# The last 32 nodes of a range as four products of 96 columns, joined by identity weights (graph network layer, one core)

## Chip, core and metric

The kernel runs on one core of one Trainium2 chip. The metric is the device time of one execution in microseconds; of several runs the median is used. The engines are TensorE (PE, its weight loads are PEld), VectorE (DVE), ScalarE (ACT), GpSimd (POOL) and SyncE (SP). SP computes nothing and issues most transfers.

## What is computed

A message-passing layer with two edge types, then a residual, then a layer normalisation over 6250 nodes of 128 features and 100000 edges, sorted by destination:

```python
Xs = X[src]
m_data = Xs @ W_data.T + b_data
m_ctrl = Xs @ W_control.T + b_control
msg = jnp.where((edge_types == 0)[:, None], m_data, m_ctrl)
agg = jax.ops.segment_sum(msg, dst, num_segments=X.shape[0])
out = agg + (X @ W_self.T + b_self)
x = _layernorm(x + relu(out), axis=-1)
```

All of it is float32 outside; the result is x.

## The kernel before

**The table.** In the first 56 us the kernel computes both messages of every node, and splits each float32 message into three bf16 parts of 128 columns (384 columns, `D3`) whose sum is the message. They stay on the chip as `m3` (98 blocks of 128 rows) and are written to memory as `table`.

**Windows.** 4320 nodes are treated in 27 windows of 160 nodes (`WN`). A window has up to 2688 edges (21 columns of 128). `ranks` sorts its edges by the table block of their source: it makes one-hot matrices (`hots`, L691), and products with `every` (all ones), `tri` and `rest` (L702) count them, so that each edge gets a slot; the list that comes out (`vs`) is written to memory as `packed` (L772) and read back for each window as `rows` (L904), spread over all partitions. Edges that find no slot are listed apart and gathered from the table (`sr`, `gl`).

**Steps.** For each window, `sums` runs 25 steps g. Stage 1 (L933): four products take 32 messages each out of four blocks of m3 into PSUM `g`, 384 columns. A cast (L436, on ACT, a few on DVE) makes `gs` of it, in bf16. Stage 2 adds the 128 messages to their nodes in the PSUM bank `a`, with a one-hot matrix `hot2` of 160 columns as weights: four products (L947) for nodes 0 to 127 of the window, 32 nodes each into partitions 32j to 32j+31, 384 columns. A bank has 512 columns, so 128 are left beside those 384 for nodes 128 to 159. Three products (L950) of 128 columns with the same 32 weights put the three bf16 parts there, one part into each of three strips of 32 partitions. At the end of the window ACT copies that corner, 96 partitions x 128 columns, into `bs`.

**Closes.** After the windows of a group (groups of 1, 2, then six times 4 windows) `close` adds the three parts (L561, on DVE), the node's own product (L518, f32) and bias (L521), and does the residual and the normalisation. The last 32 nodes of up to four windows are put together as one block of rows `f`. There one product per window (L552) adds the three parts by a 96x32 weight `fold`, three identity matrices above each other, in f32.

**Gathered nodes.** The other 1930 nodes go another way: GpSimd gathers their messages from the table, 128 edges at a time (`t_msg`, L1027, 263 of these), and TensorE adds them with one-hot weights (L1034, bank `ga`, four products of 384 columns). These sets stand between the steps of the windows.

**Order.** All instructions are entered into a `Plan` with an engine, a duration, a due time and dependences. The planner then lays them out on a model of the engines, by readiness and due time, and emits each engine's instructions in that order. The durations given to it decide only the order. `slack` on an operation makes it ready later in the plan, so that it stands further back in its queue; SP operations of some kinds have it (`packed_b` 2.0), but only when due after 60 us (`FROM`).

Of the kernel before, what the change touches and what calls it, by code (L numbers as in the profile page):

```python
# [10 lines left out]
F32 = mybir.dt.float32  # L11
# [5 lines left out]
SP = mybir.EngineType.SP  # L17
# [4 lines left out]
P = 128  # L22
D = 128
D3 = 3 * D
# [19 lines left out]
R = 32  # L44
# [203 lines left out]
def sums_over_windows(ctx, tc, x, xt, edges, w, bias, out, total):  # L248
    nc = tc.nc
    V, A, G, T, S = nc.vector, nc.scalar, nc.gpsimd, nc.tensor, nc.sync  # L250
    dram = ctx.enter_context(tc.tile_pool(name="dram", bufs=1, space=DRAM))
    const = ctx.enter_context(tc.tile_pool(name="consts", bufs=1))
    work = ctx.enter_context(tc.tile_pool(name="work", bufs=2))
# [3 lines left out]
    add = plan.add  # L257
# [4 lines left out]
    def B(pool, shape, dtype, name, bufs=1, room=None):  # L262
        return Buf(plan, pool, shape, dtype, name, bufs, room)

    def C(shape, dtype, name):
        return Buf(plan, const, shape, dtype, name, 1)

    XC = 4 * WN
    T0 = 36.0
    TW = 13.0  # L270
    LAT = 0.1
# [2 lines left out]
    SPD = 0.45  # L274
# [6 lines left out]
        lat=4.0)  # L281
    w_sb = C([D, D3], F32, "w_sb")
# [14 lines left out]
    def vec(due, cols, fn, r, w, rate=1.04):  # L297
        return add("DVE", dve(cols, rate), fn, due, r, w)
# [11 lines left out]
    ident = C([P, P], F32, "ident")  # L310
# [31 lines left out]
        [tri_f], [rest])  # L342
    every = C([P, P], BF16, "every")
    vec(4, P, lambda: V.memset(every.t, 1.0), [], [every], 0.3)
    fold = C([3 * R, R], F32, "fold")
    vec(30, R, lambda: V.tensor_add(fold.t, ident.t[: 3 * R, 0:R], ident.t[: 3 * R, R : 2 * R]),
        [ident], [fold])
    vec(30, R, lambda: V.tensor_add(fold.t, fold.t, ident.t[: 3 * R, 2 * R : 3 * R]),
        [ident, fold], [fold])
    minus = C([P, P], BF16, "minus")  # L350
    vec(1.5, P, lambda: V.tensor_scalar_mul(minus.t, ident.t, -1.0), [ident], [minus])
    wbase = C([P, NW], I32, "wbase")
# [123 lines left out]
    for q in range(NS):  # L476
        bs = range(2 * q, min(2 * q + 2, NB))
        nb = len(bs)
        due = 4.0 + MS * q
# [44 lines left out]
    def close(tag, n0, step, rows, sums_a, block, due, queues=("SP",)):  # L524
# [12 lines left out]
        if block:  # L537
            xb = B(work, [D, len(block), W4], F32, "xb", 2, 4 * W4)
            b0, b1_ = block[0][0] - P, block[-1][0] + R
            for j, (at, _) in enumerate(block):  # L540
                add("SP", SPD, lambda at=at, j=j: S.dma_start(
                    xr.t[R * j : R * j + R, nw, :], x[at : at + R, :]), due - 20, late,
                    [(xr, ("x", nw + j))], lat=2.5)
            add("SP", SPD, lambda: S.dma_start(
                xb.t, xt[:, b0:b1_].rearrange("d (b p) -> d b p", p=WN)[:, :, P:]), due - 20, late,
                [xb], lat=2.5)
            f = low()

            def mms():
                o = lambda j, m: f.t[R * j : R * j + R, :D]  # L550
                for j, (_, bs) in enumerate(block):
                    T.matmul(o(j, R), fold.t, bs.t, start=True, stop=False, skip_group_check=True)  # L552
                own(o, lambda j, m: xb.t[:, j, :], mb)
            add("PE", 0.6, mms, due, [xb, w_sb, one3, brows, fold] + [b for _, b in block], [f])
        mv = B(work, [P, nb, 2], F32, "mv" + tag, 2, 10)
        for k in range(nb):
            if k < nw:
# [63 lines left out]
    def ranks(gi, w0, nw, when, step, engines):  # L621
# [75 lines left out]
                        op=ALU.is_equal), [st1, iota1_b], [hkey(k)], 0.52)  # L697
        wide = nw * NT

        def add_to(c, wt, k, start, stop):  # L700
            for j in range(4):
                T.matmul(acc.t[R * j : R * j + R, c * wide : c * wide + wide],  # L702
                         wt.t[:, R * j : R * j + R], one(k).rearrange("p w c -> p (w c)"),
                         start=start, stop=stop, skip_group_check=True)
        mine = lambda r: [(c, c * L + r) for c in range(nc_) if c * L + r < min(KT, c * L + L)]
        for k in range((nc_ - 1) * L):
            add("PE", (nc_ - 1 - k // L) * wide / 2400, lambda k=k: [
                add_to(c, every, k, k == 0 and c == 1, False) for c in range(k // L + 1, nc_)], when + 1.5,
                [hkey(k), every], [acc])
        for r in range(L):  # L710
            due = when + 2 + step * r
            m = mine(r)
# [57 lines left out]
        def put():  # L770
            if both:
                S.dma_start(packed[gi, :both].rearrange("h p c -> p h c"), vs.t[:, :both])  # L772
            if both < nh:
                S.dma_start(packed[gi, both, :64], vs.t[:64, both])
        add("SP", SPD, put, d2 + 1, [vs], [(packed_b, gi)], lat=2.0)
        to_d = B(work, [P, nw, NS, 2], BF16, "to_d", 2, 4 * NS * 2)
        for t in range(4):
            nx = NS if t < 2 else NS - 1
# [115 lines left out]
    def sums(gi, w0, nw, placed):  # L894
# [5 lines left out]
        for i in range(nw):  # L900
# [25 lines left out]
            for g in range(NS):  # L926
# [18 lines left out]
                def stage2(g=g, gs=gs, a=a, hot2=hot2, last=last):  # L945
                    for j in range(4):
                        T.matmul(a.t[R * j : R * j + R, :D3], hot2.t[:, g, R * j : R * j + R],  # L947
                                 gs.t, start=g == 0, stop=False, skip_group_check=True)
                    for c in range(3):
                        T.matmul(a.t[R * c : R * c + R, D3:], hot2.t[:, g, P:],  # L950
                                 gs.t[:, c * D : (c + 1) * D], start=False, stop=last,
                                 skip_group_check=True)
                add("PE", 0.22, stage2, d + 0.9, [gs, (hot2, (g >= 9) + (g >= 17))], [a])
                if g == 12:
                    def own_a(i=i, a=a, xc=xc):
                        own(lambda j, m: a.t[R * j : R * j + R, :D],
                            lambda j, m: xc.t[:, i * WN + R * j : i * WN + R * j + R], P)
                    add("PE", 0.3, own_a, d + 1, [xc, w_sb, one3, brows], [a])
            bs = B(work, [3 * R, D], F32, "bs", 5)
            evict(lambda bs=bs: bs.t, lambda a=a: a.t[: 3 * R, D3:], D, due + TW + 0.8, [a], [bs])  # L960
            got.append((w0 + i, a, due + TW + 0.8, bs))
        return got

# [263 lines left out]
```

## Time and profile before

| | |
|---|---|
| median of 14 runs | 481.54 us (476.09 to 488.06) |
| profiled execution | 482.4 us, span 480.8 us |
| granted TensorE clock, mean | 0.989 |
| TensorE busy 0 to 12 us / 12 to 60 / 60 to 180 / 180 to 420 / 420 to 460 | 5.6 of 12 / 47.8 of 48 / 107.9 of 120 / 233.4 of 240 / 39.6 of 40 us |
| VectorE busy 60 to 180 / 180 to 420 / 420 to 460 | 107.8 of 120 / 209.3 of 240 / 21.3 of 40 us |
| L950: records | 1944 with gs and 81 with gl |
| L436: casts of gs | 639, 481 ns each |
| L1027: gathers | 263, 1073 ns each |

A line of the groups reads: line, engine, operation, output<-inputs, (partitions x elements, type), xcount | busy us, mean ns of one | idle us of the engine just before them, and what ended it. `128*32` is the part of TensorE's array that a product uses, rows by outputs. Products are pipelined: the next begins before the one before has ended, so their durations overlap. A line of the chain or the timeline reads: start us, duration us, engine and line, xcount, and in brackets the idle time before it. An f32 product is two records.

### The profile page before, as it was taken

Reading aid. Unit: us, or ns where it says so; the run is one execution under the profiler, and the core shown is the slowest. Engines: PE = TensorE matmul, PEld = TensorE weight load, DVE = VectorE, ACT = ScalarE, POOL = GpSimd, SP = SyncE. Lnnn points to the kernel's source line nnn. Section 1 sums busy time; section 2 is a strip of 40 time slices with the busy share of each in tenths; the row PEclk is TensorE's granted clock in tenths of the full one; section 3 lists DMA queues with packets and bytes.
Section 4 is the critical chain, followed back from the end, with each engine's and each line's share of the span. In section 5 each row is a group of like instructions: output and inputs, shape, how many; then the busy total and the mean of one; then the engine's idle time right before and its main releaser. Section 6 shows DMA issues by size and latency. Waiting matters only on the chain.

```text
span 480.8 us, 26926 instructions
## 1 busy us (share of the span) xinstructions
PE 443.3 (92%) x11461; PEld 362.0 (75%) x11461; DVE 394.5 (82%) x1271; ACT 354.2 (74%) x891; POOL 302.1 (63%) x290
## 2 busy tenths in 40 slices
PE   4999978997999799999999999999999999999990
PEld 3666556775888578788887879888888888888970
DVE  6699979998999958999988898888978779564342
ACT  2475765765877777778886789877887778989981
POOL 1100028777777777777777775777777757777700
PEclk9999999999999989999999999999999999999996
DMA  5479977428463646642766435753366534646210
GB/s 146 126 246 358 291 238 187 119 77 279 130 187 79 201 109 204 173 137 72 232 186 169 111 110 181 202 188 104 81 218 186 170 76 111 218 150 187 79 52 20
DMA packets 63117, 76.83 MB, mean 160 GB/s; under 512 B 21000, under 2 KB 52893, under 8 KB 62989
## 3 DMA queue, kind: packets, MB, share of 16 engines
q1 hardware_dynamic: 49147, 47.35, 31.3%
q0 software_dynamic: 13456, 27.42, 21.1%
q8 instruction: 91, 1.49, 1.3%
q10 hardware_dynamic: 386, 0.26, 0.2%
q14 instruction: 37, 0.30, 0.2%
HBM read 60.50 MB, written 13.17 MB: 153 GB/s over the span
## 4 chain that ended last, share of the span: by engine, by line
PE 75%; DVE 8%; ACT 7%; DMA 6%; issue 2%; ACTq 0%; DVEq 0%; POOLq 0%
PE g L933 21%; PE a L947 20%; PE rk L702 8%; PE ga L1034 7%; ACT gs L436 3%; PE a L950 3%; PE g L493 3%; PE vt L752 3%; DMA t_msg<-table,t_idx 2%; DMA rows<-packed 2%; DVE slot L716 2%; PE a L493 2%; ACT to_d L443 2%; DVE hot L920 2%; PE ga L702 1%
## 5 line engine op out<-in xcount | busy, mean ns | idle before, releaser
L1027 POOL DMA_INDIRECT t_msg<-table,t_idx x263 | 282.3, 1073 | 132.4 <-DVE hots L691 45.3
L436 ACT CAST gs<-g 128x384 bf16<-128x384 f32 x639 | 274.2, 481 | 77.6 <-PE g L933 53.3
L947 PE MATMUL a<-gs,hot 128*32 128x384 bf16 x2592 | 250.1, 330 | 7.8 <-ACT gs L436 5.0
L933 PE MATMUL g<-m,rows 128*32 128x384 bf16 x2646 | 254.6, 328 | 2.0 <-DVE rows L912 1.1
L933 PEld LDWEIGHTS <-rows 128*32 128x32 bf16 x2646 | 167.9, 135 | 14.3 <-issue 1.8
L950 PE MATMUL a<-gs,hot 128*32 128x128 bf16 x1944 | 158.4, 219 | 0.0
L947 PEld LDWEIGHTS <-hot 128*32 128x32 bf16 x2700 | 115.6, 95 | 34.4 <-issue 15.3
L1034 PE MATMUL ga<-t_msg,t_hot 128*32 128x384 bf16 x1036 | 101.5, 328 | 4.3 <-DMA t_msg<-table,t_idx 4.2
L716 DVE TENSOR_REDUCE slot<-rk 128x4 f32<-128x392 f32 (+1 forms) x138 | 76.6, 555 | 14.7 <-PE rk L702 11.7
L950 PEld LDWEIGHTS <-hot 128*32 128x32 bf16 x2025 | 81.2, 97 | 3.6
L920 DVE TENSOR_TENSOR hot<-iota_b,to_d 128x1280 bf16<-128x1280 bf16 (+1 forms) x81 | 67.4, 843 | 0.0
L702 PE MATMUL rk<-hots,tri 128*32 128x392 bf16 (+1 forms) x588 | 59.8, 317 | 0.0
L702 PE MATMUL rk<-hots,rest 128*32 128x392 bf16 (+1 forms) x556 | 54.3, 320 | 4.0 <-DVE slot L716 4.0
L1034 PEld LDWEIGHTS <-t_hot 128*32 128x32 bf16 x1036 | 49.4, 97 | 9.4 <-issue 6.0
L912 DVE TENSOR_SCALAR rows<-rows,pid 128x1568 bf16<-128x1568 bf16 x54 | 35.2, 657 | 8.1 <-DMA rows<-packed 8.0
L691 DVE TENSOR_TENSOR hots<-iota_b,st 128x784 bf16<-128x784 bf16 (+1 forms) x83 | 39.1, 489 | 0.2
L1021 DVE TENSOR_TENSOR t_hot<-iota_b,t_code 128x768 bf16<-128x768 bf16 (+2 forms) x47 | 24.6, 524 | 14.4 <-PE ga L1034 14.3
L702 PEld LDWEIGHTS <-rest 128*32 128x32 bf16 x624 | 24.7, 96 | 13.1 <-issue 10.7
L561 DVE TENSOR_REDUCE s<-a 128x128 f32<-128x384 f32 x27 | 15.0, 557 | 23.8 <-ACT bs L436 11.8
L702 PEld LDWEIGHTS <-tri 128*32 128x32 bf16 x672 | 28.1, 97 | 2.1
L752 PEld LDWEIGHTS <-two 128*64 128x64 bf16 x567 | 14.4, 109 | 8.5 <-DVE two L743 3.3
L861 POOL DMA_INDIRECT sr<-table,at x14 | 15.8, 1126 | 4.3 <-issue 2.4
(188 smaller groups left out, 531.6 us busy)
## 6 DMA issues: line engine op xcount, KB each, us to landing
rows<-packed SPq DMA_DIRECT2D x27, 784.0 KB
table<-m SPq DMA_DIRECT2D x12, 768.0 KB
t_msg<-table,t_idx POOLq DMA_INDIRECT x263
rows<-in_xt SPq DMA_DIRECT2D x8, 256.0 KB
xc<-in_xt SPq DMA_DIRECT2D x6, 320.0 KB
gl<-sr SPq DMA_DIRECT2D x27, 48.0 KB
xr<-in_x SPq DMA_DIRECT2D x5, 256.0 KB
out<-xr SPq DMA_DIRECT2D x5, 256.0 KB
```

The costliest lines, as they stand in the source:

```text
L436: [("ACT", act(cols), lambda: A.copy(o(), src())), ("DVE", dve(cols), lambda: V.tensor_copy(o(), src()))], None, None, due, r, w, lat)
L691: lambda k=k, kn=kn, ci=ci, hs4=hs4: V.tensor_tensor(hv(ci)[:, k - ks[ci] : k - ks[ci] + kn].rearrange("p k w (c d) -> p (k w) c d", d=2), ...
L702: T.matmul(acc.t[R * j : R * j + R, c * wide : c * wide + wide], wt.t[:, R * j : R * j + R], one(k).rearrange("p w c -> p (w c)"), start=s ...
L716: vec(due, len(m) * wide, lambda r=r, m=m: V.tensor_reduce(slot.t[:, r:KT:L, :], acc.t[:, : len(m) * wide].rearrange("p (k w c) -> p k w c ...
L752: T.matmul(vv()[q : q + 64, i // 2, :], two.t[:, (k - k0) * nw + i].rearrange("p f r -> p (f r)"), one(k)[:, i, :], start=k == 0 and i < 2 ...
L912: add("DVE", dve(half * NT, 0.335), lambda sp=sp, rs=rs: V.tensor_scalar(sp.t[:, rs], sp.t[:, rs], pid1.t, None, op0=ALU.is_equal), due - ...
L920: lambda i=i, hot2=hot2, s4=s4, c0=c0, c1=c1: V.tensor_tensor(hot2.t[:, c0:c1].rearrange("p g (c d) -> p g c d", d=2), iota1_b.t.rearrange ...
L933: T.matmul(gp.t[R * t : R * t + R, :D3], sp.t[:, :, 4 * g + t], m3.t[:, 4 * g + t, :], start=True, stop=True)
L947: T.matmul(a.t[R * j : R * j + R, :D3], hot2.t[:, g, R * j : R * j + R], gs.t, start=g == 0, stop=False, skip_group_check=True)
L950: T.matmul(a.t[R * c : R * c + R, D3:], hot2.t[:, g, P:], gs.t[:, c * D : (c + 1) * D], start=False, stop=last, skip_group_check=True)
L1027: add("POOL", GC, lambda m=m, kk=kk: G.indirect_dma_start(out=m.t, out_offset=None, in_=table[:, :], in_offset=bass.IndirectOffsetOnAxis(a ...
L1034: T.matmul(ga.t[R * i : R * i + R, :D3], hot.t[:, k % KB, R * i : R * i + R], m.t, start=k == 0, stop=False, skip_group_check=True)
```

## The change

It has four parts.

1. Stage 2 puts the last 32 nodes as four products of 96 columns (`Q = D3 // 4`) into all four strips of 32 partitions, instead of three of 128 columns into three strips. So 96 of the 128 columns beside the 384 are used, on all 128 partitions. `bs` is [128, 96].
2. In `close` the parts no longer lie one under the other with the same columns: a quarter of 96 columns crosses the borders between the parts of 128. Each block takes six f32 products, with the 32 columns of the identity matrix `ident` that select a strip as weights, of 96, 32, 64, 64, 32 and 96 columns. `fold` and its two VectorE instructions go.
3. The products with `every` for one one-hot matrix, one for each of up to three chains, become one product that reads the same columns up to three times.
4. The put of `packed` for group 1 gets a slack of 3.0 in the plan. Two durations in the plan change: stage 2 from 0.22 to 0.206, the close's products from 0.6 to 1.0.

```diff
+    Q = D3 // 4
...
-    fold = C([3 * R, R], F32, "fold")
-    vec(30, R, lambda: V.tensor_add(fold.t, ident.t[: 3 * R, 0:R], ident.t[: 3 * R, R : 2 * R]),
-        [ident], [fold])
-    vec(30, R, lambda: V.tensor_add(fold.t, fold.t, ident.t[: 3 * R, 2 * R : 3 * R]),
-        [ident, fold], [fold])
...
-                for j, (_, bs) in enumerate(block):
-                    T.matmul(o(j, R), fold.t, bs.t, start=True, stop=False, skip_group_check=True)
+                first_ = True
+                for at in sorted({*range(0, D3, Q), *range(0, D3, D)}):
+                    q, f0 = at // Q, at % D
+                    n = min(Q - at % Q, D - f0)
+                    for j, (_, bs) in enumerate(block):
+                        T.matmul(f.t[R * j : R * j + R, f0 : f0 + n],
+                                 ident.t[:, R * q : R * q + R],
+                                 bs.t[:, at % Q : at % Q + n], start=first_, stop=False,
+                                 skip_group_check=True)
+                    first_ = False
                 own(o, lambda j, m: xb.t[:, j, :], mb)
-            add("PE", 0.6, mms, due, [xb, w_sb, one3, brows, fold] + [b for _, b in block], [f])
+            add("PE", 1.0, mms, due, [xb, w_sb, one3, brows, ident] + [b for _, b in block], [f])
...
-        def add_to(c, wt, k, start, stop):
+        def add_to(c, wt, k, start, stop, n=1):
             for j in range(4):
-                T.matmul(acc.t[R * j : R * j + R, c * wide : c * wide + wide],
-                         wt.t[:, R * j : R * j + R], one(k).rearrange("p w c -> p (w c)"),
-                         start=start, stop=stop, skip_group_check=True)
+                T.matmul(acc.t[R * j : R * j + R, c * wide : (c + n) * wide].rearrange(
+                    "p (n c) -> p n c", n=n), wt.t[:, R * j : R * j + R],
+                    one(k).rearrange("p w c -> p (w c)")[:, None, :].to_broadcast([P, n, wide]),
+                    start=start, stop=stop, skip_group_check=True)
...
         for k in range((nc_ - 1) * L):
-            add("PE", (nc_ - 1 - k // L) * wide / 2400, lambda k=k: [
-                add_to(c, every, k, k == 0 and c == 1, False) for c in range(k // L + 1, nc_)], when + 1.5,
-                [hkey(k), every], [acc])
+            more = nc_ - 1 - k // L
+            add("PE", max(more * wide / 2400, 0.08), lambda k=k, more=more: add_to(
+                nc_ - more, every, k, k == 0, False, more), when + 1.5, [hkey(k), every], [acc])
...
-        add("SP", SPD, put, d2 + 1, [vs], [(packed_b, gi)], lat=2.0)
+        op = add("SP", SPD, put, d2 + 1, [vs], [(packed_b, gi)], lat=2.0)
+        if gi == 1:
+            op.slack = 3.0
...
-                    for c in range(3):
-                        T.matmul(a.t[R * c : R * c + R, D3:], hot2.t[:, g, P:],
-                                 gs.t[:, c * D : (c + 1) * D], start=False, stop=last,
+                    for c in range(4):
+                        T.matmul(a.t[R * c : R * c + R, D3 : D3 + Q], hot2.t[:, g, P:],
+                                 gs.t[:, c * Q : c * Q + Q], start=False, stop=last,
                                  skip_group_check=True)
-                add("PE", 0.22, stage2, d + 0.9, [gs, (hot2, (g >= 9) + (g >= 17))], [a])
+                add("PE", 0.206, stage2, d + 0.9, [gs, (hot2, (g >= 9) + (g >= 17))], [a])
...
-            bs = B(work, [3 * R, D], F32, "bs", 5)
-            evict(lambda bs=bs: bs.t, lambda a=a: a.t[: 3 * R, D3:], D, due + TW + 0.8, [a], [bs])
+            bs = B(work, [P, Q], F32, "bs", 5)
+            evict(lambda bs=bs: bs.t, lambda a=a: a.t[:, D3 : D3 + Q], Q, due + TW + 0.8, [a], [bs])
```

In the queues this gives: SP's put of `packed` for group 1 stands behind the third of the small xr loads (L541), and not ahead of the first xr load; both reads of `rows` of group 1 remain behind it, past one xb and one t_xc load. From 60 us on places change in all queues; GpSimd's gathers keep their order, and sr reads shift by one to three places among them.

## The prediction

> **What bounds the kernel now.** I read the page first, then the chain of waits, the waits, the timeline of three stretches, and the busy time by stage.
>
> ```profile
> span 480.8 us, 26926 instructions
> PE 443.3 (92%) x11461; PEld 362.0 (75%) x11461; DVE 394.5 (82%) x1271; ACT 354.2 (74%) x891; POOL 302.1 (63%) x290
> PE 75%; DVE 8%; ACT 7%; DMA 6%; issue 2%; ACTq 0%; DVEq 0%; POOLq 0%
> L947 PE MATMUL a<-gs,hot 128*32 128x384 bf16 x2592 | 250.1, 330 | 7.8 <-ACT gs L436 5.0
> L950 PE MATMUL a<-gs,hot 128*32 128x128 bf16 x1944 | 158.4, 219 | 0.0
> ```
>
> TensorE is busy for 92% of the span and holds 75% of the chain. The mean of 219 ns of L950 is no price, since four such products run beside each other and one follows another before it ends. The price is read from starts, in the timeline of PE in a dense stretch:
>
> ```profile
> 444.31 0.44 PE L947 MATMUL a<-gs,hot 128*32 128x384 bf16 x4
> 444.69 0.43 PE L947 MATMUL a<-gs,hot 128*32 128x384 bf16 x4
> 445.02 0.48 PE L1034 MATMUL ga<-t_msg,t_hot 128*32 128x384 bf16 x4
> 445.23 0.44 PE L947 MATMUL a<-gs,hot 128*32 128x384 bf16 x4
> 445.61 0.43 PE L947 MATMUL a<-gs,hot 128*32 128x384 bf16 x4
> ```
>
> A step g (four L933, four L947, three L950) takes 0.38 us; with a gathered set (L1034, four products of 384 columns) between, 0.54. So a set of four times 384 columns costs 0.16 us, which is 0.417 ns a column, and a step is 384 + 384 + 128 columns: 0.16 + 0.16 + 0.055 = 0.375. Three of the four strips of 32 outputs carry all 896 columns; the fourth has 768. The change takes the three full strips to 864.
>
> But not all of the span is of this kind. Three pieces of the chain between 157 and 169 us, then a line of the waits (total, times, longest, in us) and one of GpSimd's timeline:
>
> ```profile
> 157.43 3.96 DMA t_msg<-table,t_idx
> 161.55 6.97 DMA t_msg<-table,t_idx
> 168.57 0.35 PE ga L1034 x4
> PE ga L1034 <- DMA t_msg<-table,t_idx: 4.2, 3, 3.4
> 68.25 1.03 POOL L1027 DMA_INDIRECT t_msg<-table,t_idx  x1 [45.34 <-DVE hots L691]
> ```
>
> GpSimd issues its first gather at 68.25 us, after the table has landed, and from there one every 1.3 to 1.4 us with 0.30 between; at 168.57 TensorE has stood 3.37 us for one of them. Whatever TensorE saves before 168.6 is lost in this wait. After it the chain (180 to 468 us) has L933 28.6%, L947 26.6%, L1034 10.0%, L702 9.0%, L950 4.0%, L752 3.1% and a few small ones of TensorE: some 85%.
>
> **The change, part by part.**
>
> *Four products of 96 columns (L950).* L950 has 2025 records with all its forms, three a step, and 1572 of them start after 168.6: 524 steps of the 675. Each step gives 32 columns x 0.417 = 13.3 ns on the strips that set the pace. 524 x 13.3 = 7.0 us; 85% of that, the share of TensorE in the chain there, is 5.9. The 151 steps before give 2.0 us into the wait of 3.37: nothing. A fourth weight load and product a step land on the strip that had room. Is a product of 96 columns with its own weights really shorter than one of 128? The nearest row has 98 columns:
>
> ```profile
> 16.32 0.36 PE L702 MATMUL ga<-xr,rest 128*32 128x98 bf16 x16
> 16.51 0.35 PE L702 MATMUL ga<-xr,tri 128*32 128x98 bf16 x16
> ```
>
> Four sets of four in 0.19 us: 47 ns a set, with sixteen weight loads, against 55 for 128. So the saving lies between 8 ns (this rounded row: 4.2 us after 168.6, 3.6 on the chain) and 13.3; I take 13.3, since the columns of the larger sets are exact to 1%.
>
> The Trainium skill speaks against it: "TensorE: Matmul & The Clock Gate", section "Back-to-back issue gap", gives about 81 ns for each matmul of 128 columns in a stream where every matmul has its own weight load. Were that the floor here, 96 columns would gain nothing and the fourth product might cost. The trace has 55 ns for 128 columns with a load each, so the rule's figure doesn't hold for these narrow strips. By the page the sum would be no gain here, and 483.7 us with the closes.
>
> *ScalarE's pace.* A cast of gs costs 0.39 us in a run of six (2.44 us at 464.72: less the 0.48 of the last, over five). That is more than a step without a gathered set, so where several such steps follow one another ScalarE sets the pace and 0.367 instead of 0.38 buys nothing. With one gathered set to three steps it is 3 x 0.38 + 0.16 = 1.30 for TensorE, 1.17 for ScalarE. ScalarE was busy for 43.3 of the last 48 us, 48 of 60 before. For this and VectorE's like waits I give back 0.9 us (bounds 0 and 3).
>
> *The identity products (L552).* Before, a close sends one f32 product of 128 columns for each block of 32 rows, four strips beside each other. The nearest price is L518, also f32, 128 columns, four strips: 0.22 us for its eight records on the chain at 426.37. After, each block takes six products with 96, 32, 64, 64, 32 and 96 columns: 384 columns, 0.66 us, 0.44 more for a close. There are seven closes with such a block, first records at 115, 182, 243, 302, 361, 420 and 468 us. The first lies before the wait. The last is hidden: TensorE has finished vt at 469.02 and VectorE takes it up at 469.85, after the sums of the last window, so 0.8 us cover it; without that cover it is 0.44 too. Five count: 2.2 us. Bounds: nothing, if they fall into waits; and if none of the twelve weight loads of a strip (110 ns each in the row of L552) hides behind a short product, 12 x 0.11 + 0.66 - 0.22 = 1.76 a close, 8.8 for five and 1.0 at the end. L518's 0.22 for two loads and two products has the loads hidden, so I stay near the first.
>
> *Fewer products with ones.* 36 sets of 98 columns become 18 of 98 to 294, the same columns. By the 47 ns of a 98-column set against its 41 ns of columns, 18 x 6 = 0.1 us at most, before 26 us, so ahead of the wait at 168.6: nothing.
>
> *The put of group 1 and the table.* SyncE's queue before:
>
> ```profile
> 62.17 0.33 SPq L772 DMA_DIRECT2D packed<-vs  x1
> 62.60 0.38 SPq L534 DMA_DIRECT2D xr<-in_x  x1
> 63.03 0.42 SPq L1011 DMA_DIRECT2D t_xc<-in_xt  x1
> 63.55 0.38 SPq L509 DMA_DIRECT2D table<-m  x1
> 64.03 0.42 SPq L534 DMA_DIRECT2D xr<-in_x  x1
> 64.50 1.92 SPq L541 DMA_DIRECT2D xr<-in_x  x1
> 66.52 0.84 SPq L904 DMA_DIRECT2D rows<-packed  x2
> ```
>
> The put of packed moves behind the third xr of L541; the two reads of rows stay behind it. What follows the put waits for the last m3 (VectorE has it at 62.56), so the table still goes at about 63.5: 0 to 0.4 us earlier, taken as 0. The put goes at about 67.4 (the first xr of L541 ends at 66.42, and two more take 0.93 together). Rows must wait until it has landed (3.04 us for another put, at 106.55): 70.4 instead of 66.52, so windows 1 and 2 begin some 3.9 us later. VectorE stood idle for 2.42 us waiting for these rows, and its new order puts hot and hots ahead of them; TensorE's set is busy on columns for about two thirds of 60 to 80 us. The slip ends at the latest in the 3.37 us at 168.57, with the 2.0 saved before: cost 0, and without that cover 3.9.
>
> *The rest.* fold leaves VectorE (two of 0.18 us, just before it idles 3.18): nothing. bs is cast as 96 columns for 128, 0.26 to about 0.24 us, 27 times, on ScalarE: inside its slack. The new costs of the planner shift places in all five queues after 60 us; I have no price for it but the size of the single waits in the trace, 0.4 to 3.4 us, and take +-2 into the range.
>
> **Sum.** 5.9 - 0.9 - 2.2 = 2.8 us less. The profiled execution took 482.4 (span 480.8): 479.6. It lies 0.9 over the median of the fourteen runs, 481.5, against which I predict 478.7.
>
> **The rivals.**
>
> *The gathers hold it.* GpSimd goes without a break from 68.25 to 457, bar a few waits for TensorE (3.5 us the longest, at 394.8). If TensorE catches up with the gathers again, its saving turns into waits in L1034. For: one such wait is there already. Against: the last gathered set starts at 463.4, 5 us or so after the last gather has landed, and GpSimd's own waits for TensorE shrink as TensorE speeds up. Half of the 5.9 gone: 481.5 - 2.9 - 0 + 2.2 = 480.8.
>
> *The put is paid for.* The slip of 3.9 us isn't covered at 168.57 because the ranks of the next group slip too. 481.5 - 2.8 + 3.9 - 2.0 = 480.6, in the same band.
>
> *The identity products cost what their weight loads cost* (the other side): 8.8 + 1.0 us in place of 2.2, so 481.5 - 5.0 + 9.8 = 486.3. It decides from 1.5 us a close on (7.5 for five eats 5.0 and passes the half per cent). For: each of the 24 products of a close loads its own f32 weights, for as little as 32 columns. Against: L518's rows.
>
> **How the numbers follow.** 0.5% is 2.4 us, about what these runs can tell from no change: faster is below 479.1, slower above 483.9. Forecast 0.52 (its own range 475.5 to 480), the gathers 0.20, the put 0.11, identity products or a bad reshuffle of that size 0.17. Of the forecast some 0.45 lie below 479.1, and 0.01 of the others: faster 0.46; slower 0.17; the rest, 0.37, the same. The range goes from 474.5 (all 7.0 us, closes in waits) to 483.5, which leaves the worse part of the last rival out.
>
> **What would show it.** L950's successor at 96 columns in groups of four, a step of 0.37 us instead of 0.38; PE's busy time down; L552 with some 324 records, taking 0.66 us a close; the wait for t_msg near 168 as long or longer, and L912 for windows 1 and 2 at about 74 us. It is wrong if a close takes over 1.5 us, if new waits in L1034 stand in the second half, or if the steps still take 0.38.

## The result, and the profile after

The changed kernel takes 495.8 us (median of 10 runs, 492.72 to 504.48), the kernel before 483.2 (47 runs): 1.0294 times as long, 95% interval 1.0262 to 1.0326. The ratios in this document compare fast runs alone, so they differ by up to 0.4% from the quotient of two medians (here 1.026). The forecast was 478.7, its range ended at 483.5. The profiled executions have spans of 496.7 and 480.8 us, 15.9 apart.

From the page of the kernel after (the groups read as those of before; L954 is the former L947, L957 the former L950, L940 the former L933):

```profile
span 496.7 us, 28664 instructions
PE 448.8 (90%) x12334; PEld 341.9 (69%) x12334; DVE 396.0 (80%) x1270; ACT 352.2 (71%) x890; POOL 303.1 (61%) x290
q8 instruction: 98, 1.61, 1.3%
PE 75%; DVE 7%; ACT 7%; issue 5%; DMA 4%; POOL 1%; SPq 0%; ACTq 0%; DVEq 0%
L954 PE MATMUL a<-gs,hot 128*32 128x384 bf16 x2592 | 231.8, 330 | 10.3 <-ACT gs L432 3.7
L940 PE MATMUL g<-m,rows 128*32 128x384 bf16 x2646 | 230.3, 339 | 7.2 <-issue 6.2
L957 PE MATMUL a<-gs,hot 128*32 128x96 bf16 x2592 | 158.6, 207 | 3.6 <-issue 3.6
L940 PEld LDWEIGHTS <-rows 128*32 128x32 bf16 x2646 | 105.9, 137 | 27.9 <-issue 6.6
```

TensorE is as large a part of the chain as before (75%), but "issue" has gone from 2% to 5%. This is time in which an engine waits for nothing that the profile shows. Among the longest pieces of the chain from 180 us on are such lines (start, duration; the first is of before, the others of after):

```profile
186.87 1.10 issue
251.74 1.54 issue
421.04 2.13 issue
```

The timeline of TensorE after shows what the second of them looks like (the bracket is the idle time before the line):

```profile
251.03 0.54 PE L940 MATMUL g<-m,rows 128*32 128x384 bf16 x8
251.37 0.37 PE L954 MATMUL a<-gs,hot 128*32 128x384 bf16 x4
253.27 0.23 PE L957 MATMUL a<-gs,hot 128*32 128x96 bf16 x4 [1.54 <-issue]
253.32 0.34 PE L706 MATMUL rk<-hots,rest 128*32 128x392 bf16 x4
```

The small products of a step stand still for 1.54 us although they read the same `gs` and the same weights tile as the products before them. I call such a stop a pause: over 0.45 us between two records of TensorE after 60 us, the later of which waits for no semaphore. There are 3 before (3.5 us in all) and 16 after (21.1 us). The granted clock is no rival of this size: its mean was 0.989 before and 0.982 after in these two executions, so that TensorE lost 5.3 and 8.9 us of full clock.

All of them stand at the same place in TensorE's stream. Count its weight loads and products from the start: in both kernels the number of records ahead of each pause leaves 187, 188 or 189 when it is divided by 256 (4284, 5308, 7100, 7868, 8892 for the first five of after). The few instructions of TensorE's sequencer that the trace lists besides (semaphores above all, 14 in after) make up the difference: counted with them, every one of the 105 pauses in the nine traces that have any, from chips where before takes about 482 us, stands exactly 193 past a multiple of 256. Why it is 193 and not 0 isn't shown. And each pause ends 1.25 to 1.6 us after a packet of queue q8 has landed. That queue's line says what these packets are: 98 packets of instructions, 1.61 MB, so 16 KB each, one for every 252 of the 24,668 records. Before, with 22,922 records, there are fewer:

```profile
q8 instruction: 91, 1.49, 1.3%
```

TensorE comes to the end of one packet of its own instructions and the next has not come.

The Trainium skill has the mechanism in "Runtime: NRT & Kernel Launch", section "Instruction fetch mechanics": a small instruction memory, filled in blocks of 16 KiB or 256 instructions, with a cost that is mostly hidden. The trace agrees on the 256. It agrees on the hiding in the kernel before, with 3.5 us of pauses; in the changed kernel they come to 21.1 us, and there the measurement decides.

Three sums from the two traces come to about the difference:

| | before | after | difference |
|---|---|---|---|
| pauses at the end of a packet, us | 3.5 | 21.1 | +17.6 |
| closes: from an L552 to the next product of another line, seven closes in all, us | 1.9 | 6.2 | +4.3 |
| gaps over 0.45 us in TensorE that do wait for a semaphore, from 60 us on | 21.4 | 15.0 | -6.4 |
| sum | | | +15.5 of 15.9 |

The step itself is no shorter. Between 180 and 450 us a step without a gathered set between has a median of 382 ns before and 381 after.

### The profile page after: what moved, and what is told of

It is laid out like the page before. It is cut to its first block, busy times and chain, and to the rows that moved or that the text cites. A ratio compares the mean times of both kernels' runs of the same rounds, so it can differ in the third digit from the quotient of the medians.

```text
span 496.7 us, 28664 instructions
## 1 busy us (share of the span) xinstructions
PE 448.8 (90%) x12334; PEld 341.9 (69%) x12334; DVE 396.0 (80%) x1270; ACT 352.2 (71%) x890; POOL 303.1 (61%) x290
## 3 DMA queue, kind: packets, MB, share of 16 engines
q8 instruction: 98, 1.61, 1.3%
## 4 chain that ended last, share of the span: by engine, by line
PE 75%; DVE 7%; ACT 7%; issue 5%; DMA 4%; POOL 1%; SPq 0%; ACTq 0%; DVEq 0%
PE g L940 22%; PE a L954 19%; PE rk L706 8%; PE ga L1041 7%; PE a L957 5%; ACT gs L432 3%; PE vt L757 3%; PE g L489 2%; ACT to_d L439 2%; DMA sr<-table,at 1%; PE a L489 1%; DVE slot L721 1%; PE a L514 1%; DMA win<-in_edges 1%; DVE hot L927 1%
## 5 line engine op out<-in xcount | busy, mean ns | idle before, releaser
L954 PE MATMUL a<-gs,hot 128*32 128x384 bf16 x2592 | 231.8, 330 | 10.3 <-ACT gs L432 3.7
L940 PE MATMUL g<-m,rows 128*32 128x384 bf16 x2646 | 230.3, 339 | 7.2 <-issue 6.2
L957 PE MATMUL a<-gs,hot 128*32 128x96 bf16 x2592 | 158.6, 207 | 3.6 <-issue 3.6
L954 PEld LDWEIGHTS <-hot 128*32 128x32 bf16 x2700 | 109.7, 98 | 43.5 <-issue 24.5
L940 PEld LDWEIGHTS <-rows 128*32 128x32 bf16 x2646 | 105.9, 137 | 27.9 <-issue 6.6
L957 PEld LDWEIGHTS <-hot 128*32 128x32 bf16 x2700 | 88.3, 97 | 16.7 <-issue 4.6
L1041 PE MATMUL ga<-t_msg,t_hot 128*32 128x384 bf16 x1036 | 84.3, 329 | 1.2 <-issue 1.2
L927 DVE TENSOR_TENSOR hot<-iota_b,to_d 128x1280 bf16<-128x1280 bf16 (+1 forms) x81 | 67.4, 845 | 0.0
L706 PE MATMUL rk<-hots,tri 128*32 128x392 bf16 (+1 forms) x588 | 49.7, 319 | 0.0
L706 PE MATMUL rk<-hots,rest 128*32 128x392 bf16 (+1 forms) x556 | 47.3, 321 | 0.9 <-DVE slot L721 0.7
L1041 PEld LDWEIGHTS <-t_hot 128*32 128x32 bf16 x1036 | 34.5, 101 | 7.6 <-issue 2.4
L706 PEld LDWEIGHTS <-rest 128*32 128x32 bf16 x624 | 18.9, 98 | 11.1 <-issue 7.5
L706 PEld LDWEIGHTS <-tri 128*32 128x32 bf16 x672 | 19.6, 99 | 2.5
```

The source lines that it names most:

```text
L706: T.matmul(acc.t[R * j : R * j + R, c * wide : (c + n) * wide].rearrange("p (n c) -> p n c", n=n), wt.t[:, R * j : R * j + R], one(k).rear ...
L927: lambda i=i, hot2=hot2, s4=s4, c0=c0, c1=c1: V.tensor_tensor(hot2.t[:, c0:c1].rearrange("p g (c d) -> p g c d", d=2), iota1_b.t.rearrange ...
L940: T.matmul(gp.t[R * t : R * t + R, :D3], sp.t[:, :, 4 * g + t], m3.t[:, 4 * g + t, :], start=True, stop=True)
L957: T.matmul(a.t[R * c : R * c + R, D3 : D3 + Q], hot2.t[:, g, P:], gs.t[:, c * Q : c * Q + Q], start=False, stop=last, skip_group_check=True)
L1041: T.matmul(ga.t[R * i : R * i + R, :D3], hot.t[:, k % KB, R * i : R * i + R], m.t, start=k == 0, stop=False, skip_group_check=True)
```

## The experiments

Where the kernel before takes about 483 us, a comparison with it stands on its own. Three of the five groups of runs fell on chips on which the kernel before itself takes 696 us. The granted clock was 0.89 to 0.92 there, in place of 0.97 to 0.99, and TensorE also stands still for some 0.7 us ahead of single instructions, at any place in a packet (114 pauses of 74.0 us in `e2_rest`). Their ratios are to the kernel before on the same chip. They tell what a part of the change costs there, but not by the pauses at the end of a packet, which their traces do not set apart. The fourth product, the three products of 96, the close and the loads in pieces were therefore run on another chip as well; the parts alone, `e17_rotate` and `e18_three_close1` were not.

### Which part of the change costs

The parts alone: `e1_only96` is the changed kernel with part 3 and the put of part 4 taken back, `e2_rest` the kernel before with these two. The two durations of part 4 go with the first.

> Parts 1 and 2 of the change alone (four products of 96, six identity products a block); the products with ones and the put of group 1 stay as before. If the fourth product of a step and the closes are the cause (theory: TensorE's instructions arrive too late), it takes 492 to 498 us, with a dozen or more pauses of 0.6 to 2.5 us in TensorE's stream that no semaphore explains. If the put or the merged products with ones carry the loss, it is within 2 us of the kernel before.

> Parts 3 and 4 alone (merged products with ones, slack for the put of group 1) on the kernel before. Instruction theory: 36 fewer sets early, steps untouched, so 479 to 485 us and about three such pauses, as before. If the put is the cause (its rival), 486 us or more, with the loss there at 80 us already.

On a chip with before at 695.9: the four products and the closes alone 1.0206 (1.0143 to 1.027), parts 3 and 4 alone 1.0037 (1.0009 to 1.0065). On this chip the put and the merged products cost little, and the loss is in parts 1 and 2. The times in microseconds that were expected can't be compared on this chip.

### The fourth product alone

```diff
-                    for c in range(3):
+                    for c in range(4):
                         T.matmul(a.t[R * c : R * c + R, D3:], hot2.t[:, g, P:],
-                                 gs.t[:, c * D : (c + 1) * D], start=False, stop=last,
+                                 gs.t[:, c % 3 * D : (c % 3 + 1) * D], start=False, stop=last,
```

> The kernel before with a fourth product of 128 columns a step, into the strip that the last 32 nodes left free; nobody reads what it writes, and the order of all other work is that of before. Column count on the slowest strips is unchanged (896). Instruction theory: 24 instead of 22 instructions a step, so ten to twenty pauses and 490 to 500 us, steps of 0.38 us between them. If only columns count (the prediction's premise that the strip had room), within 1 us of before. If it is the short product that hurts (theory of the uncovered weight load), within 1 us of before too, with L940/L933 products after a small product staying at 326 ns.

> The kernel of e3_four128 once more, because there the kernel before itself took 695.9 us on that chip and not 483. Judged by the ratio to before on the same chip. Instruction theory: 1.015 to 1.035 where before takes about 483, with ten to twenty pauses in TensorE's stream that follow no semaphore; only columns count: 1.00.

`e3_four128`: 1.0112 (1.0076 to 1.0148) on the chip with before at 695.9. `e5_four128`: 493.2 us against 483.2, 1.0242 (1.0155 to 1.033). This is the kernel before in everything, with one more product on the strip that nobody used, and it costs 10 us by the medians. Its timeline:

```profile
429.10 0.35 PE L933 MATMUL g<-m,rows 128*32 128x384 bf16 x4
429.27 0.34 PE L947 MATMUL a<-gs,hot 128*32 128x384 bf16 x2
430.82 0.34 PE L947 MATMUL a<-gs,hot 128*32 128x384 bf16 x2 [1.21 <-issue]
430.82 0.23 PE L950 MATMUL a<-gs,hot 128*32 128x128 bf16 x2
```

Two of the four products of one set are issued, and the two others 1.5 us later: no tile can be the reason, they all read the same `gs`. There are 9 pauses, 9.2 us, again at 188 or 189 over a multiple of 256. They are one fewer than the ten to twenty that were expected. At the same place stand stops at which a semaphore was waited for too: with these it is 11 stops of 12.9 us, against 5 of 5.2 us in before. The difference of 7.7 us is most of the 8.5 between the spans of the two traces (489.3 and 480.8). Between them a step still takes 381 ns, so the columns had room on that strip; the instructions had none. The granted clock was 0.988, against 0.989.

### Three products of 96, and the closes

`e4_three96` and `e6_three96`: `for c in range(3 if g else 4)` in the changed kernel.

> The changed kernel without the fourth product of 96 columns in 24 of the 25 steps (the last 96 of the 384 summed columns of the last 32 nodes, all in the lowest bf16 part, keep only one step's share); order as in the changed kernel. Instruction theory: 22 instructions a step as before, three to five pauses left, so 480 to 486 us, with the closes 3 us dearer than before included. Uncovered weight load: a step still takes 0.38 us and stage 1 products after a small product 339 ns. If neither the count nor the fourth product matters, it stays at 494 to 497.

> The kernel of e4_three96 once more, for the same reason. Instruction theory: 0.995 to 1.01 of before, three to five pauses. Uncovered weight load: steps of 0.38 us all the same, stage 1 products after a small one at 339 ns.

`e4_three96`: 1.0169 (1.0124 to 1.0214) with before at 695.9. `e6_three96`: 491.8 against 483.2, 1.021 (1.0125 to 1.0295). Expected was at most 1.01. With the instructions of a step as before, 9 pauses of 12.3 us remain. Three of them begin 3.9 to 4.4 us behind the first product of a close (pauses at 247.4, 308.6 and 368.7 us, closes at 243.5, 304.2 and 364.8), and the packets ahead of them lasted only 3.6 to 3.9 us. So the step's count alone was not the cause, and the closes were tried next: `for at in [0]` in place of the six columns, in the changed kernel.

> The changed kernel with one of the six identity products of each block in a close (the first, 96 columns): five sixths of the sum of the last 32 nodes are left out. 540 of the 648 instructions of these products go. If closes cost what their records span (0.6 to 1.15 us each, 3.4 us over the seven) and also empty the instruction queue, pauses within 2 us after a close go (in the changed kernel four or five of them, some 7 us), and the time falls to 0.98 to 0.99 of the changed kernel's, so 1.01 to 1.02 of before. If closes lie beside other work and only the step's count matters, 1.025 to 1.03 of before.

> The kernel of e11_close1 once more, because there before itself took 696.6 us. In the changed kernel TensorE's pauses without a semaphore sum to 21 us, in before to 3.5, with the fourth product alone (e5_four128) to 9, with three products and the new closes (e6_three96) to 12. If fourth product and closes each add their share, leaving out five of six close products brings the pauses to 9 to 13 us, the closes to 0.3 us each, and the time to 1.005 to 1.02 of before. If the closes' instructions do not empty the queue, pauses stay at 18 to 24 us and the time at 1.02 to 1.03.

`e11_close1`: 1.0173 (1.0153 to 1.0194) with before at 696.6. `e13_close1`: 489.5 against 481.7, 1.0163 (1.0098 to 1.0228), with 10 pauses of 12.4 us, as expected. Without five sixths of the closes' products the changed kernel is 1.3% nearer to before (1.0294 less 1.0163, 6.3 us of 482; by the two intervals some 3.5 us either way), of which the closes themselves are about 4 us by the traces (2.2 in place of 6.2 for the seven). The traces alone would make it more, with spans of 484.8 and 496.7, but the one of `e13_close1` is of the fastest of its four runs. A close sends 96 loads and products in about 0.7 us (48 records of each), where a step sends 24 in 0.38.

Both undone together:

> The changed kernel without the fourth product in 24 of 25 steps and with one of six close products (both left out as in e6_three96 and e13_close1): 22 instructions a step and fewer close instructions, with the merged products with ones, the later put and the changed order kept. If added instructions are the whole cause: pauses of 2 to 6 us, 0.995 to 1.005 of before. If the order or the put has a share: 1.01 or more, with pauses as few.

1.011 (1.0069 to 1.015), with before at 696.5. So some 1.1% remains there, of which parts 3 and 4 explain 0.4 (`e2_rest`). The rest, 0.7%, is not settled: the planner's new order, the small products of 96 columns and the one close product that stays were not tried one by one. On a chip where before takes 482 us this kernel was not run, so whether the pauses of packets would all be gone there is not shown.

### Why the step did not get shorter

In the changed kernel a stage 1 product takes 338 ns in the median, before it took 326; and it is 339 right behind a set of small products and 326 behind nearly any other. The set of four products of 96 columns takes 43 ns, and the load of `rows` weights 137, against 98 for those of `hot`. `e7_small_first` puts the small products first:

```diff
+                    for c in range(4):
+                        T.matmul(a.t[R * c : R * c + R, D3 : D3 + Q], hot2.t[:, g, P:],
+                                 gs.t[:, c * Q : c * Q + Q], start=g == 0, stop=False,
...
                     for j in range(4):
                         T.matmul(a.t[R * j : R * j + R, :D3], hot2.t[:, g, R * j : R * j + R],
-                                 gs.t, start=g == 0, stop=False, skip_group_check=True)
+                                 gs.t, start=False, stop=last, skip_group_check=True)
```

> The changed kernel with the four products of 96 columns ahead of the four of 384 in stage 2, so that a long product precedes stage 1 and covers the load of its weights. Uncovered weight load: stage 1 products fall from 339 to 326 ns and a step between pauses from 0.38 to 0.367 us; with the pauses unchanged (the instruction count is that of the changed kernel) the time falls by at most 6 us, to 1.015 to 1.03 of before, or not at all if the shorter step only empties the instruction queue sooner. If the load is not the cause, steps stay at 0.38 us.

Stage 1 products take 326 ns and the step 368. In its timeline (L954 are now the small products, L958 the large ones):

```profile
452.53 0.23 PE L954 MATMUL a<-gs,hot 128*32 128x96 bf16 x4
452.57 0.35 PE L958 MATMUL a<-gs,hot 128*32 128x384 bf16 x4
452.74 0.35 PE L940 MATMUL g<-m,rows 128*32 128x384 bf16 x4
452.90 0.23 PE L954 MATMUL a<-gs,hot 128*32 128x96 bf16 x4
```

From 452.53 to 452.90 is 0.37: the 13 ns of the prediction are there. The time isn't: 496.3 against 483.2, 1.0282 (1.018 to 1.0384). There are 15 pauses of 23.0 us. One stands right behind a close:

```profile
367.81 0.86 PE L552 MATMUL vt<-bs,ident 128*32 128x96 f32 x48
368.49 0.40 PE L514 MATMUL vt<-w_sb,xb 128*32 128x128 f32 x8
...
368.98 0.34 PE L958 MATMUL a<-gs,hot 128*32 128x384 bf16 x4
372.27 0.39 PE L940 MATMUL g<-m,rows 128*32 128x384 bf16 x4 [2.96 <-issue]
```

The products of the close use 96 of the packet's 256 instructions in 0.7 us, and TensorE stands for 2.96 us at its end. With a shorter step the end of a packet only comes sooner.

### Fewer instructions at any price

`e8_one_wide`: `T.matmul(a.t[:, :D3], hot2.t[:, g, :P], gs.t, ...)` in place of the four large products of stage 2.

> The changed kernel with one product of 128 outputs in stage 2 in place of four of 32 outputs for nodes 0 to 127 (the same sums, 6 instructions a step less: 18 instead of 24). Instruction theory: the pauses go (none to three), and if a wide product follows the narrow ones at no loss, 475 to 485 us where before takes 483. If a change of the width costs something (a load of 128 weights that nothing covers, or strips that must empty first), a step is 0.05 to 0.15 us longer and the time 510 to 570 us, with no pauses.

603.0 against 483.2, 1.2493 (1.2397 to 1.2589).

```profile
499.90 0.34 PE L953 MATMUL a<-gs,hot 128*128 128x384 bf16 x1
500.17 0.23 PE L956 MATMUL a<-gs,hot 128*32 128x96 bf16 x4
500.22 0.35 PE L940 MATMUL g<-m,rows 128*32 128x384 bf16 x4
500.50 0.34 PE L953 MATMUL a<-gs,hot 128*128 128x384 bf16 x1
```

(Timeline of TensorE; L953 is the wide product, L956 the small ones.) No pause is left, as expected with 18 instructions a step. But the step takes 0.60 us: the large product holds up its successor for 0.27 where a set of four holds it for 0.16, and stage 1 is followed after 0.28 in place of 0.16. That is 0.22 us more a step, where 0.05 to 0.15 had been thought of. Whether it is the change of the width or the load of 128 weights was not told apart; either way it costs more than all the pauses.

### When does a packet come late?

For each packet the traces give the time from the place where TensorE takes up the packet before it to the landing of the next (between 100 us and 40 us before the end; medians, with pauses and gathered sets included):

| | before | after |
|---|---|---|
| packet in use, 70 and 78 packets | 4.61 us | 4.30 us |
| next packet lands after, SyncE's queue moving under 100 KB in 3.5 us (31 and 43 packets) | 1.85 us | 1.83 us |
| the same, over 700 KB in 3.5 us (10 and 15 packets) | 4.01 us | 4.12 us |
| packets that land after more than 3 us | 9 | 17 |

In steps alone, without gathered sets, 256 instructions at 22 a step of 0.38 us would last 4.42 us, at 24 a step 4.05 (an estimate from the steps; the expectations call a packet in use a page). The landing and the 1.25 to 1.6 us after it must fit in. Beside a large load, 4 + 1.4 does not fit in either kernel, and a packet that lasts a little longer hides more of it. That more packets also landed late after the change is measured, but not explained. The large loads are mostly `rows` (784 KB each, L904/L911). Would smaller pieces let the packet through?

```diff
-            for j in range(RP):
+            for j in range(4):
...
-                    sp.t[P // RP * j : P // RP * (j + 1)].rearrange("p r c -> p (r c)"),
+                    sp.t[:, R // 4 * j : R // 4 * (j + 1)].rearrange("p r c -> p (r c)"),
```

> The changed kernel with each load of rows (784 KB, 6272 bytes a partition) issued as four loads of 1568 bytes a partition. Theory: a packet of 256 TensorE instructions lands about 1.9 us after TensorE takes up the page before it when SyncE's queue moves little, and 3.5 to 5 us when such a load runs; 24 instructions a step use up a page in 4.05 us and so wait. If the packet stands behind long pieces of the load, four short ones let it through sooner: pauses fall from 21 us to 5 to 12, time 0.98 to 0.99 of the changed kernel's, so 1.01 to 1.02 of before. If it is the bandwidth that is short, pauses and time stay (1.025 to 1.035 of before). Rival (pauses have nothing to do with the loads): the same as the latter, with pauses at the same places.

> The kernel before with the same four loads. Its pauses are 3.5 us in three places; if the short pieces help, they go and it takes 0.99 to 1.00 of before; if 81 more issues on SyncE delay other loads, up to 1.02.

> Small products first (as e7_small_first, step 0.368 us) together with the four loads. If both theories hold, steps of 0.368 us and pauses down to 5 to 12 us: 480 to 488 us, 0.995 to 1.01 of before. If the loads in pieces do not help, 1.025 to 1.03 as e7_small_first.

> The kernel of e9_rows4 once more (changed kernel, each load of rows in four pieces of 1568 bytes a partition). If the pieces let an instruction packet through sooner or spread the bytes: packets that land over 3 us after their page fall from 15 to under 9, pauses from 21 to 8 to 14 us, time 1.005 to 1.02 of before. If not: 1.025 to 1.035.

> The kernel of e10_before_rows4 once more. If the pieces help, before's three pauses go and the time is 0.99 to 1.00 of before; if not, 0.998 to 1.01.

> The kernel of e12_first_rows4 once more (small products first, so steps of 0.368 us, and loads in four pieces). If the pieces help: 0.99 to 1.015 of before, with pauses of 8 to 15 us. If not, 1.02 to 1.035, as e7_small_first.

With before at 696.6 us: `e9_rows4` 1.0249 (1.0214 to 1.0285), `e10_before_rows4` 0.9973 (0.9951 to 0.9996), `e12_first_rows4` 1.0228 (1.0159 to 1.0297). With before at 481.7: `e14_rows4` 503.7 us, 1.0428 (1.0358 to 1.0498); `e15_before_rows4` 492.2, 1.0188 (1.0133 to 1.0243); `e16_first_rows4` 505.2, 1.0503 (1.0435 to 1.0572). The last three are slower than was expected even if the pieces did nothing. The pauses are 16 with 23.1 us, 10 with 12.1 and 17 with 23.5; packets that land over 3 us after the one before them is taken up are 23 (17 without the pieces), 16 (9) and 19 (19). The remedy fails, on the kernel before too, where 10 pauses stand in place of 3. That a packet lands late while SyncE's queue moves much is measured; that shorter pieces would let it through is refuted; what holds it up stays open. The added waits for four loads in place of one (59 instructions of TensorE's sequencer in place of 14) give a check of another kind: by records alone the pauses of `e14_rows4` move from 182 past a multiple of 256 down to 146, and counted with those instructions all stand at 193. A version with fewer bytes in these loads wasn't tried.

### The same columns with no instruction more

The sum of the last 32 nodes may collect any part in any strip, since the close adds all of them. `e17_rotate` uses this in the kernel before:

```diff
+    def strips(cols, k=4):
+        js = sorted(range(4), key=lambda j: (load[j], j))[:k]
+        for j in js:
+            load[j] += cols
+        return js
...
-                    for c in range(3):
-                        T.matmul(a.t[R * c : R * c + R, D3:], hot2.t[:, g, P:],
+                    for c, j in enumerate(strips(D, 3)):
+                        T.matmul(a.t[R * j : R * j + R, D3:], hot2.t[:, g, P:],
```

> The kernel before, with its three products of 128 columns for the last 32 nodes, but at each step in the three strips that have had the fewest columns, so that the fourth strip takes part too; the products of each other set stand in the order of the strips' columns; bs has 128 partitions and fold adds four identities, one product a block as before. On the average 864 columns a strip as in the changed kernel, but 22 instructions a step and the close of before. If strips may run apart by 128 columns and instructions are the limit: a step of 0.365 to 0.37 us on the average, pauses of 4 to 9 us (a page of 256 instructions now lasts 4.3 us), 474 to 482 us where before takes 482, 0.985 to 1.00. If a set cannot start until all strips are free: steps stay at 0.38 us and the time within 0.5% of before. If it is the columns' balance that costs in the changed kernel, 1.01 or more.

0.9978 (0.9952 to 1.0004), on a chip with before at 696.5. Three sets of stage 2 in its timeline:

```profile
650.31 0.35 PE L956 MATMUL a<-gs,hot 128*32 128x384 bf16 x4
...
650.69 0.35 PE L956 MATMUL a<-gs,hot 128*32 128x384 bf16 x4
...
651.07 0.35 PE L956 MATMUL a<-gs,hot 128*32 128x384 bf16 x4
```

They begin 0.38 us apart, as before, and the median of the steps is 0.386. A shorter step can be seen on such a chip: with the small products first (`e12_first_rows4`) 82 of 192 steps take 0.36 to 0.372 us, here 15 of 207. So in this run a strip that skips its small product doesn't run on into the next step, and equal columns over several steps bring nothing. No version that was run is shown to beat the kernel before (`e10_before_rows4` had 0.9973 on one chip, and the same kernel 1.0188 on another).

## Why the prediction was wrong, step by step

**The bound** was read rightly: TensorE is 90% busy and 75% of the chain after the change too. But the price list had only columns and loads in it. "Issue" stood in the chain of before with 2%, with a piece of 1.10 us at 186.87, and I did not ask what it was.

**Four products of 96 columns.** Here the forecast failed, at the sentence that a fourth weight load and product a step "land on the strip that had room", priced at nothing. The fourth product alone costs 10 us (`e5_four128`, 1.0242), none of it on the strip, where the step stays at 381 ns: it makes 24 instructions of 22, so that a packet of 256 is used up sooner (4.30 us in place of 4.61 in the changed kernel) while the next takes up to 5.8 to land. The other half of the step, 13.3 ns a step, was possible, but did not come in this order: 43 ns of small products in front of stage 1 leave its products at 338 ns. With the small products first the step is 368 ns, 13 less (`e7_small_first`). That the load of the `rows` weights is no longer covered would fit its 137 ns, and that 128 columns (55 ns) leave 326 ns in `e5_four128`; it was not measured by itself, so the cause of these 13 ns is argued and not shown. The 81 ns of the Trainium skill ("TensorE: Matmul & The Clock Gate", section "Back-to-back issue gap") for a product of 128 with its own load, which were weighed against this step, do not hold for these strips after the change either (43 ns for four of 96). The sum by that page, 483.7, lay nearer to the measured time than the forecast; that is luck, since the time went elsewhere.

**ScalarE's pace**, 0.9 us given back, can't be judged: the step that should have met it did not come.

**The identity products.** Taken at 0.44 us more a close, with bounds of 0 and 1.76; measured is 0.61 in the mean ((6.2 - 1.9) / 7), and 2.9 us for the five that were counted in place of 2.2. The fourth close, in the timeline of TensorE after:

```profile
309.15 0.25 PE L552 MATMUL vt<-bs,ident 128*32 128x96 f32 x2
309.20 0.96 PE L552 MATMUL vt<-bs,ident 128*32 128x96 f32 x46
310.21 0.43 PE L514 MATMUL vt<-w_sb,xb 128*32 128x128 f32 x8
```

This close takes 1.06 us, the dearest in the middle; the point of 1.5 us from which the third rival was to decide is not reached by any. But the rival was nearer than the forecast in another way: five sixths of these products cost 6.3 us in all (`e13_close1`, with the wide interval given above), and the pauses fall from 21.1 to 12.4 us without them, since 96 instructions in 0.7 us also use up a packet. The prediction counted their loads as time on a strip, never as instructions.

**Products with ones, the put, the table.** Taken at nothing; alone they cost 0.4% on a chip with before at 695.9 (`e2_rest`). The slip was 1.1 us for the load of rows, not 3.9:

```profile
66.09 0.37 SPq L777 DMA_DIRECT2D packed<-vs  x1
67.65 0.81 SPq L911 DMA_DIRECT2D rows<-packed  x2
```

(SyncE's timeline of after.) The put goes at 66.09 and not 67.4, and the reads of `rows` at 67.65, against 66.52 before; VectorE compares them from 73.2 us on, against 70.8. The wait of 3.37 us for a gather at 168.57, which was to swallow this, is gone, and one of the same length stands at 80.8 to 84.2 us, by the waits of TensorE (total, times, longest):

```profile
PE a L954 <- DMA gl<-sr: 3.4, 1, 3.4
```

So the gain of the first 168 us had no wait to vanish into, but there was no gain.

**The rivals.** The gathers did not hold the kernel: no wait for t_msg is left on TensorE, which came to all of them after the gathers had landed. None of the three rivals names the instructions. The slower side had 0.17 and the range ended at 483.5; a mechanism that was not on the list (17.6 us more of pauses) was worth more than the sum of all that were.

**What would show it**, by the prediction's own list: L957 has 96 columns in fours, as it said. The step stayed at 0.38, which it named as a sign of being wrong. TensorE's busy time went up, 443.3 to 448.8. L552 has 324 records as forecast.

## What to carry to other kernels

Where an engine is bound, count its instructions per microsecond as well as its columns: a product that fills an idle strip is free only if its weight load and it can be supplied. Look for idle time put down to "issue", and whether it recurs at a fixed number of instructions; if it does, the kernel is already near that limit, and bursts of small products cost more than their own time. And a short product must be judged with the one behind it: here the order of the two decided whether the step became shorter.

## What the runs showed of the hardware that was not expected

- TensorE's instructions came in packets of 16 KB, and TensorE stopped at their borders, 187 to 189 records past a multiple of 256 in most kernels, and exactly 193 past one in all nine traces when the sequencer's instructions are counted too, for up to 2.96 us by the timeline. Where 256 instructions lasted 7.0 us in the median and the next packet landed after 4.2 us at the latest (`e8_one_wide`), there was no such stop.
- At a pause of before or after, the landed packet was taken up 1.25 to 1.6 us after its landing.
- Four products of 96 columns on four strips took 43 ns; stage 1 products behind them 339 ns, behind 128 columns or 384 columns 326.
- One product of 128 outputs among sets of four with 32 outputs made the step 0.60 us in place of 0.38.
- The same kernel took 481 to 483 us on some chips and 696 on others. On the latter the clock was granted at half in 16 stretches, 128 us together (`e2_rest`; three stretches, 20 us, in after). The waits of TensorE's loads that follow nothing in the profile are 125.1 us there for one line alone (before: 15.3 us for that line, L947):

```profile
PEld L950 <- issue: 125.1, 183, 4.8
```

That is `e2_rest` (line, total, times, longest). The pauses on these chips go with the instructions too: 101 to 115 of them in the kernels with 22 a step, 133 to 144 in those with 24. What makes these chips slower was not found.
